# One weight load issued later, an addition moved from VectorE to GpSimd, four small transposes one block earlier, and one product of zeros fewer

## The chip, the cores and the metric

The kernel runs on one core of a Trainium2 chip. A core has five engines that run side by side, each with its own queue of instructions that it takes in order: TensorE (PE in the profile, with its weight loads shown apart as PEld), VectorE (DVE), ScalarE (ACT), GpSimd (POOL) and SyncE (SP). Transfers between the chip's main memory (HBM) and the on-chip memory are started by an instruction in one of these queues and then run on the core's 16 DMA engines. The metric is the time of one execution in microseconds (us) of the core.

## The reference

The inputs are x (8 batches of 1024 rows of 512), a condition row of 512 for each batch, and weights. Two layers are applied one after the other, each with a residual connection. Cut to what matters:

```python
ae = _layernorm(ada_emb, ln_g, ln_b)                  # 8 x 512
h = jax.nn.gelu(ae @ w1 + b1, approximate=False)      # 8 x 512
xw = h @ w2 + b2                                      # 8 x 8192
x_a, x_b = jnp.split(xw, 2, axis=-1)                  # each 8 x 512 x 8
layer = base_layer[None] + jnp.einsum('bdr,bkr->bdk', x_a, x_b)
x = x + (x + jnp.einsum('btc,bco->bto', x, layer))    # first layer
ys = y * scale                                        # y is the condition row
d = jax.lax.rsqrt(jnp.einsum('bi,io->bo', ys * ys, weight * weight) + EPS)
x = x + jnp.einsum('bsi,io->bso', x * ys[:, None, :], weight) * d[:, None, :]
```

The first layer is x(2I + base + a low-rank term), the second is x(I + diag(ys) W diag(d)), where I is the identity. So for each batch the kernel first makes one 512x512 matrix, P = (2I + base + low rank)(I + diag(ys) W diag(d)), and then multiplies the 1024 rows of x by it.

## The kernel before

**Tiling.** All 512-wide matrices are held as four chunks of 128 rows (one chunk for each set of 128 partitions). A product of two float32 matrices is made of three products in a shorter float format: each factor is split into a rounded part ("h", written by ScalarE as a copy or a scaled copy) and a rest ("l", written by VectorE as the difference), and h·h, h·l and l·h are summed in the accumulators.

**Stages.** A head of some 26 us loads the weights, makes the split of base (with 2I added) and of W, the layer norm of the condition, the gelu, and the first of the matrices. A middle part makes the other matrices while w2 streams in; then the main part multiplies x by them, 128 rows at a time, with the matrices for later batches made in between; the last batches use a seven-product scheme. TensorE works through all of these in one fixed order.

**What sets the order.** In the head nearly every instruction goes through a wrapper (`ve`, `se`, `sy` for VectorE, ScalarE, SyncE; `mm` and `turn` for TensorE; `pin` in general) that keeps each engine's instructions in the order in which they stand in the kernel. `nc.gpsimd` instructions are not wrapped unless `pin` is written around them. Waits between engines are put in by the framework from the data that the instructions read and write.

**The names that the change touches.**

- `w_sb` holds W. Its chunks 0 and 1 are loaded by two transfers from ScalarE's queue (lines 89 and 90), ahead of ScalarE's load of its function table and its first small activation (`root`, line 124). Chunks 2 and 3 come in one transfer from SyncE's queue.
- `b_raw` holds the transpose of base; chunks 0, 1 and then 2 with 3 are loaded from SyncE's queue. `sm` is a small block with the norm's gains, the transposed condition, and a 128x128 identity, `ident`.
- `twice_i(k)` (line 154) adds 2I to the diagonal 128x128 block of chunk k of `b_raw`. `round_b(k)` (line 158) is ScalarE's rounded copy `bh`, `rest_b(k)` VectorE's rest `bl`. `round_yw(k)` and `rest_yw(k)` do the same for diag(ys) W of batch 0 (tiles `nh` and `nl`, n0 in the kernel).
- For chunk 0 the rounding is done in three pieces: columns 128 to 255, 256 to 511, and last the diagonal block, columns 0 to 127 (lines 181 to 183). TensorE's first products take the four column blocks in the order 1, 2, 3, 0 (line 263), so that the fourth product is the first that needs the diagonal block.
- `keep_warm` (line 112) gives TensorE products of a tile of zeros, from about the start of the program until the first real operands are there; `WARM` says how many.
- `pg` are the four accumulators of the first product; `first_base(k, cs)` adds chunk k to the column blocks cs, three products for each. `RowsProduct(ysq, wsq, "v")` is a row product for d; it makes `pq_v`, ScalarE copies that to `q_v`, and `rv.turn()` transposes it (`pt_v`).
- `pa` receives the transposes of the normalised condition, `ae` (line 274; `ae` is a slice of the tile `drow`, and is called drow in the profile). VectorE makes `aeT` from it, and `aeT` feeds the next row product, `pq_z`.

Of the kernel before, what the change touches and what calls it, by code (L numbers as in the profile page):

```python
# [7 lines left out]
F32 = mybir.dt.float32  # L8
F32R = mybir.dt.float32r
AF = mybir.ActivationFunctionType  # L10
ALU = mybir.AluOpType
# [3 lines left out]
P = 128  # L15
# [8 lines left out]
D_EPS = 1e-8  # L24
SCALE = float(1.0 / D ** 0.5)
NFILL = 4
WARM = 12


@with_exitstack  # L30
def cond_resid_kernel(ctx: ExitStack, tc: tile.TileContext, small, cond, condrows, consts,
# [10 lines left out]
    nc = tc.nc  # L42
# [4 lines left out]
    def turn(*args):  # L47
        tc.keep_in_program_order(nc.tensor.transpose(*args))

    pin = tc.keep_in_program_order  # L50
# [13 lines left out]
    ve, se, sy = InOrder(nc.vector), InOrder(nc.scalar), InOrder(nc.sync)  # L64
# [12 lines left out]
    sp = setup.enter_context(tc.tile_pool(name="sp", bufs=1))  # L77
# [5 lines left out]
    w_sb = cp.tile([P, KC, D], F32, name="w_sb")  # L83
# [2 lines left out]
    xab = sp.tile([P, D], F32, name="xab")  # L86
    drow = sp.tile([P, D], F32, name="drow")
    cnd, ae = xab[:NB, :], drow[:NB, :]
    for k in range(2):
        se.dma_start(w_sb[:, k, :], weight[:, k, :])  # L90
    sy.dma_start(sm, small)
    for k in range(2):
        sy.dma_start(b_raw[:, k, :], baseT[:, k, :])
# [8 lines left out]
    ident = sm[:, 44:44 + P]  # L102
# [9 lines left out]
    def keep_warm(count):  # L112
        for _ in range(count):
            mm(warm.rearrange("p (a c) -> p a c", c=P), zero,
               zero.unsqueeze(1).to_broadcast([P, D // P, P]), start=True, stop=True)

    keep_warm(WARM)
    eps_d = cp.tile([P, 1], F32, name="eps_d")
# [3 lines left out]

    root = cp.tile([NB, 1], F32, name="root")
    se.activation(root, eps_l, AF.Sqrt)


    hT = sp.tile([P, KC, 2, 32], F32, name="hT")
    nc.gpsimd.memset(hT, 0.0)

    bh = cp.tile([P, KC, D], F32R, name="bh")  # L130
    bl = cp.tile([P, KC, D], F32R, name="bl")
# [13 lines left out]
    def round_yw(k):  # L145

        se.mul(n0[k][0], w_sb[:, k, :], ysT[:, k, 0:1])

    def rest_yw(k):
        h, l = n0[k]  # L150
        ve.scalar_tensor_tensor(l, w_sb[:, k, :], ysT[:, k, 0:1], h.bitcast(F32),
                                           ALU.mult, ALU.subtract)

    def twice_i(k):
        blk = b_raw[:, k, k * P:(k + 1) * P]
        ve.scalar_tensor_tensor(blk, ident, 2.0, blk, ALU.mult, ALU.add)

    def round_b(k, lo=0, hi=D, by=se.copy):
        (by(bh[:, k, lo:hi], b_raw[:, k, lo:hi]))
# [17 lines left out]

    ve.tensor_scalar_mul(ysT, condT, SCALE)
    twice_i(0)
    round_yw(0)  # L180
    round_b(0, P, 2 * P)
# [3 lines left out]
    rest_b(0)  # L185
    round_yw(1)
    twice_i(1)
    round_b(1)
    rest_yw(1)
# [11 lines left out]
    ve_l = sp.tile([NB, 1], F32, name="ve_l")  # L201
    ve.tensor_scalar(ve_l, mv[:, 1:2], 1.0, LN_EPS, ALU.mult, ALU.add)
    twice_i(2)
    twice_i(3)
    r, t = newton_rsqrt(ve_l, sd, [NB, 1], "l")
# [4 lines left out]
    def base_mms(ps, c, k, nhl, last):  # L210
        h, l = nhl
        for i, (s, m) in enumerate(((bh, h), (bh, l), (bl, h))):
            mm(ps, s[:, k, c * P:(c + 1) * P], m, start=(k == 0 and i == 0),
               stop=(last and k == KC - 1 and i == 2))
# [3 lines left out]
    def first_base(k, cs=range(KC)):  # L218
        for c in cs:
            base_mms(pg[c], c, k, n0[k], True)  # L220
# [43 lines left out]
            mm(pg[c], s[:, 0, c * P:(c + 1) * P], m, start=(i == 0), stop=False)  # L264
    first_base(1, (0, 1))
    round_yw(2)
    round_b(2)
    rest_yw(2)
    round_yw(3)
    rv = RowsProduct(ysq, wsq, "v")  # L270
    rv.keep()
    round_b(3)
    first_base(1, (2, 3))
    pa = misc.tile([P, KC, NB], F32, tag="misc", name="pa")
    for k in range(KC):
        turn(pa[:, k, :], ae[:, k * P:(k + 1) * P], ident[:NB, :NB])
    aeT = sp.tile([P, KC, 4, NB], F32, name="aeT")
    ve.tensor_mul(aeT, pa.unsqueeze(2).to_broadcast([P, KC, 4, NB]),
                  lng.unsqueeze(2).unsqueeze(3).to_broadcast([P, KC, 4, NB]))
# [915 lines left out]
```

## Time and profile before

| | |
|---|---|
| median of 3 runs | 294.32 us (294.32 to 295.01) |
| the profiled execution's own time | 294.56 us |
| its span in the profile | 292.8 us |
| TensorE busy | 287.9 us, 98% of the span |
| VectorE busy | 215.1 us, 73% |
| ScalarE busy | 175.0 us, 60% |
| GpSimd busy | 33.6 us, 11% |

The profile is of one execution. Its span runs from the first instruction to the last; the execution's own time is 1.76 us longer. "Busy" counts the time in which an engine works on an instruction, without the issue of transfers from SyncE and ScalarE. Ends of TensorE's products are modelled, so the distance between starts tells more than a duration.

### The profile page before, as it was taken

Reading aid. Unit: us, or ns where it says so; the run is one execution under the profiler, and the core shown is the slowest. Engines: PE = TensorE matmul, PEld = TensorE weight load, DVE = VectorE, ACT = ScalarE, POOL = GpSimd, SP = SyncE. Lnnn points to the kernel's source line nnn. Section 1 sums busy time; section 2 is a strip of 40 time slices with the busy share of each in tenths; the row PEclk is TensorE's granted clock in tenths of the full one; section 3 lists DMA queues with packets and bytes.
Section 4 is the critical chain, followed back from the end, with each engine's and each line's share of the span. In section 5 each row is a group of like instructions: output and inputs, shape, how many; then the busy total and the mean of one; then the engine's idle time right before and its main releaser. Section 6 shows DMA issues by size and latency. Waiting matters only on the chain.

```text
span 292.8 us, 4096 instructions
## 1 busy us (share of the span) xinstructions
PE 287.9 (98%) x1520; PEld 225.9 (77%) x1520; DVE 215.1 (73%) x299; ACT 175.0 (60%) x272; POOL 33.6 (11%) x72
## 2 busy tenths in 40 slices
PE   8999999999999999999999999999999999999995
PEld 3655566557877778888877888887888889999994
DVE  2789988989926999618799565325789976797912
ACT  4757254186858884748653575544658745846741
POOL 0011000202944551000023000000000000000000
PEclk9999999999999999999999999999999999999999
DMA  7999999993699784342428114252275870852334
GB/s 215 410 427 418 407 373 387 405 363 113 179 323 322 208 271 133 92 162 79 172 74 251 72 72 121 96 210 75 75 251 172 291 257 0 290 204 85 143 146 143
DMA packets 19924, 62.14 MB, mean 212 GB/s; under 512 B 2736, under 2 KB 4016, under 8 KB 15552
## 3 DMA queue, kind: packets, MB, share of 16 engines
q1 hardware_dynamic: 9504, 43.76, 40.2%
q10 hardware_dynamic: 6912, 12.32, 11.6%
q0 software_dynamic: 3488, 5.79, 7.5%
q8 instruction: 12, 0.20, 0.3%
q14 instruction: 8, 0.07, 0.1%
HBM read 44.02 MB, written 17.84 MB: 211 GB/s over the span
## 4 chain that ended last, share of the span: by engine, by line
PE 98%; DVE 0%; ACT 0%; issue 0%; ACTq 0%
PE po L45 42%; PE pp L45 20%; PE sw L45 9%; PE px L45 5%; PE sz L45 5%; PE pq L45 4%; PE pg L45 4%; PE sv L45 2%; PE warm L45 2%; PE pr L45 1%; PE pt_t L45 1%; PE ps_t L45 0%; PE pq_z L45 0%; PE pq_v L45 0%; ACT o L62 0%; DVE o L62 0%
## 5 line engine op out<-in xcount | busy, mean ns | idle before, releaser
L45 PE MATMUL po<-ph,xs 128*128 128x512 f32 x352 | 113.8, 393 | 0.0
L45 PEld LDWEIGHTS po<-ph,xs 128*128 128x128 f32 x352 | 66.1, 188 | 15.6 <-issue 1.7
L45 PE MATMUL po<-pl,xs 128*128 128x512 f32 x176 | 68.7, 390 | 0.0
L62 ACT COPY o<-po 128x512 f32<-128x512 f32 x44 | 25.9, 588 | 35.3 <-PE po L45 35.3
L45 PEld LDWEIGHTS po<-pl,xs 128*128 128x128 f32 x176 | 33.1, 188 | 6.7
L62 DVE TENSOR_TENSOR xs<-x,xs 128x1024 fp32r<-128x1024 f32 (+1 forms) x23 | 26.9, 1175 | 14.9 <-ACT xs L62 14.9
L62 DVE TENSOR_TENSOR nl_p<-n,nh_p 128x1024 fp32r<-128x1024 f32 x21 | 25.6, 1221 | 12.4 <-ACT nh_p L62 12.4
L62 ACT CAST nh_p<-n 128x1024 fp32r<-128x1024 f32 x21 | 22.1, 1053 | 13.0 <-DVE n L62 10.7
L62 ACT CAST xs<-x 128x1024 fp32r<-128x1024 f32 x22 | 23.0, 1056 | 3.4 <-DMA x<-in_x 3.4
L62 ACT COPY q<-pp 128x512 f32<-128x512 f32 x30 | 17.4, 586 | 8.8 <-PE pp L45 8.6
L539 POOL DMA_DIRECT2D fa<-kept_a x28 | 13.8, 512 | 58.4 <-PE pr L45 54.1
L45 PE MATMUL pp<-nh_p,sh 128*128 128x512 f32 x48 | 19.1, 397 | 0.0
L45 PE MATMUL pp<-nl_p,sh 128*128 128x512 f32 x48 | 18.8, 391 | 0.0
L45 PE MATMUL pp<-nh_p,sl 128*128 128x512 f32 x48 | 18.8, 391 | 0.0
L62 ACT CAST sh<-sraw 128x1024 fp32r<-128x1024 f32 (+1 forms) x14 | 12.9, 926 | 6.8 <-DVE sraw L62 6.8
L62 DVE SCALAR_TENSOR_TENSOR n<-w_sb,ysT,d 128x512 f32<-128x512 f32 x24 | 16.9, 746 | 0.0
L62 DVE TENSOR_TENSOR sl<-sraw,sh 128x1024 fp32r<-128x1024 f32 (+1 forms) x14 | 15.0, 1068 | 2.2 <-ACT sh L62 2.2
L62 DVE TENSOR_TENSOR pl<-q,ph 128x1024 fp32r<-128x1024 f32 (+1 forms) x10 | 11.1, 1116 | 7.0 <-ACT ph L62 6.9
L45 PE MATMUL px<-w,hT 128*32 128x512 f32 x128 | 15.6, 599 | 0.0
L62 ACT COPY o<-sw 128x512 f32<-128x512 f32 (+1 forms) x12 | 6.2, 518 | 15.4 <-PE sw L45 12.3
L62 DVE TENSOR_TENSOR q<-pr,q 128x512 f32<-128x512 f32 x14 | 8.8, 685 | 8.1 <-PE pr L45 8.0
L62 DVE TENSOR_TENSOR n<-n,n 128x1024 f32<-128x1024 f32 x12 | 14.5, 1222 | 0.1
(198 smaller groups left out, 576.9 us busy)
## 6 DMA issues: line engine op xcount, KB each, us to landing
w<-in_w SPq DMA_DIRECT2D x16, 1024.0 KB, 9.9
x<-in_x SPq DMA_DIRECT2D x16, 1024.0 KB, 5.5
out<-o ACTq DMA_DIRECT2D x44, 256.0 KB, 2.5
out<-o SPq DMA_DIRECT2D x8, 512.0 KB, 3.0
fa<-kept_a POOLq DMA_DIRECT2D x28, 64.0 KB, 2.8
ft<-kept_t POOLq DMA_DIRECT2D x28, 64.0 KB, 3.3
d<-d_out POOLq DMA_DIRECT2D x6, 256.0 KB, 7.7
w_sb<-in_w SPq DMA_DIRECT2D x1, 1024.0 KB, 8.4
```

The lines of the kernel that those rows point to most:

```text
L45: tc.keep_in_program_order(nc.tensor.matmul(*args, **kw))
L62: return lambda *a, **kw: pin(f(*a, **kw)) if InOrder.on else f(*a, **kw)
L539: nc.gpsimd.dma_start(fold[name, b][32 * c:32 * c + 32, :], kept[name, g][32 * i:32 * i + 32, :])
```

## The change

Four edits, all in the head:

- Of the two transfers of W on ScalarE's queue the second, chunk 1, is now issued behind the table load and the activation `root`.
- GpSimd makes a tile `two_i` = I + I once, and `twice_i` becomes an addition of that tile on GpSimd, for all four chunks. VectorE had done it with one multiply-and-add.
- The four transposes into `pa` are moved ahead of the last block (three products) of `first_base(1)`. In the text, `RowsProduct` and its copy `q_v` also move ahead of `round_b(2)` and `round_yw(3)`. On TensorE the row product stays where it was; on ScalarE the copy `q_v` now comes before the rounding of chunk 2.
- `WARM` goes from 12 to 11.

```diff
-WARM = 12
+WARM = 11
...
-    for k in range(2):
-        se.dma_start(w_sb[:, k, :], weight[:, k, :])
+    se.dma_start(w_sb[:, 0, :], weight[:, 0, :])
...
     se.activation(root, eps_l, AF.Sqrt)
+    se.dma_start(w_sb[:, 1, :], weight[:, 1, :])
...
     nc.gpsimd.memset(hT, 0.0)
+    two_i = sp.tile([P, P], F32, name="two_i")
+    pin(nc.gpsimd.tensor_tensor(two_i, ident, ident, ALU.add))
...
     def twice_i(k):
         blk = b_raw[:, k, k * P:(k + 1) * P]
-        ve.scalar_tensor_tensor(blk, ident, 2.0, blk, ALU.mult, ALU.add)
+        pin(nc.gpsimd.tensor_tensor(blk, blk, two_i, ALU.add))
...
     round_yw(2)
-    round_b(2)
     rest_yw(2)
-    round_yw(3)
     rv = RowsProduct(ysq, wsq, "v")
     rv.keep()
+    round_b(2)
+    round_yw(3)
     round_b(3)
-    first_base(1, (2, 3))
+    first_base(1, (2,))
     pa = misc.tile([P, KC, NB], F32, tag="misc", name="pa")
     for k in range(KC):
         turn(pa[:, k, :], ae[:, k * P:(k + 1) * P], ident[:NB, :NB])
+    first_base(1, (3,))
```

In the built program GpSimd's queue holds one instruction more than the text: between the clearing of `hT` and the making of `two_i` stands a reload of GpSimd's library of code (library number 0). It waits for nothing. The program before has no such instruction: there GpSimd only clears, copies and issues transfers.

## The prediction

> **What bounds the kernel now.** I read the page first, then the chain that ended last, then the first 15 us in order of time, engine by engine, because the diff touches nothing later. The page:
>
> ```profile
> span 292.8 us, 4096 instructions
> PE 287.9 (98%) x1520; PEld 225.9 (77%) x1520; DVE 215.1 (73%) x299; ACT 175.0 (60%) x272; POOL 33.6 (11%) x72
> PE 98%; DVE 0%; ACT 0%; issue 0%; ACTq 0%
> ```
>
> TensorE carries 98% of the span and 98% of the chain. So nothing done on another engine shortens the kernel unless TensorE starts earlier or loses an idle moment, and whatever lets TensorE idle in the head is added to the end almost whole: the 265 us behind the head have no slack to give it back. The chain in order of time, for the head:
>
> ```profile
> 0.99 5.30 PE warm L45 x12
> 6.29 4.50 PE pg L45 x18
> 10.79 0.99 PE pq_v L45 x8
> ...
> 13.38 0.34 PE pa L48 x4
> 13.72 0.60 PE pt_v L48 x4
> 14.32 0.15 issue
> 14.47 1.07 PE pq_z L45 x8
> ```
>
> TensorE runs without a break from 0.99, and the only idle moment here that the diff can reach is the 0.15 ahead of pq_z, where the transposes feed aeT. The other engines in that stretch, in order of time:
>
> ```profile
> 0.73 0.31 POOL L128 MEMSET hT<- 128x256 f32 x1 [0.29 <-POOLq L1187]
> 1.66 1.28 ACT L62 ACT_TABLE_LOAD   x1 [1.66 <-PEq L1187]
> 3.86 0.18 DVE L62 TENSOR_SCALAR ysT<-sm 128x32 f32<-128x32 f32 x1 [2.92 <-DMA sm<-in_small]
> 5.69 0.81 ACT L62 CAST bh<-b_raw 128x128 fp32r<-128x128 f32 x3 [0.59 <-DMA b_raw<-in_baseT]
> 6.40 0.72 ACT L62 ACTIVATE nh<-w_sb,ysT 128x512 fp32r<-128x512 f32 x1
> 7.48 0.62 ACT L62 CAST bh<-b_raw 128x512 fp32r<-128x512 f32 x1 [0.36 <-DVE b_raw L62]
> 10.21 0.49 DVE L62 SCALAR_TENSOR_TENSOR b_raw<-sm,b_raw 128x128 f32<-128x128 f32 x2 [0.21 <-DMA b_raw<-in_baseT]
> 15.60 0.40 POOL L745 CAST onesb<-cst 128x256 fp32r<-128x256 f32 x1 [14.55 <-DMA cst<-in_consts]
> ```
>
> and the weight loads of TensorE between 5.5 and 7.4:
>
> ```profile
> 6.04 1.05 PEld L45 LDWEIGHTS pg<-nh,bh 128*128 128x128 f32 x4 [0.66 <-ACT bh L62]
> 7.13 0.42 PEld L45 LDWEIGHTS pg<-nl,bh 128*128 128x128 f32 x2
> ```
>
> Base chunk 0 lands at about 5.65. ScalarE then rounds its three pieces; looked at one by one they start at 5.69, 5.90 and 6.20 (0.29 us for the last, the diagonal block). The first four real weight loads start at 6.04, 6.35, 6.63 and 6.90. The first two follow the first two pieces within 0.06; the fourth, which needs the diagonal block, comes 0.41 after that piece is done. From there TensorE goes at 0.23 a product.
>
> **Fewer zeros.** The twelve zero products start 0.43 apart, the last at 5.65, so TensorE is free at 6.08, just when the first rounded piece is there. Without one it is free at 5.65. What that is worth hangs on base chunk 0 landing earlier: nothing if it does not, 0.43 at most.
>
> **W chunk 1 later.** ScalarE's two issues took 0.89, the table load 1.28, root 0.20. The second issue moves from 1.2 to about 0.73 + 0.45 + 1.28 + 0.20 = 2.66, 1.5 later; its own 0.43 on ScalarE falls into that engine's 1.23 wait for W chunk 0. The pair landed 4.1 after issue in the mean, the first 3.6, so the second 4.6, at 5.8. It would now land between 5.8 (if the queue had held it back anyway) and 7.3. Its reader is the scaled copy nh at 6.40, behind which bh, four squares, sd and the norm stand on ScalarE. At 7.3 the copy of base chunk 1 would start at 8.0 instead of 7.48, and VectorE's two rests would end at about 9.45, where TensorE wants the second one at 9.46. So the delay costs nothing to 0.1, and covers itself with the two rests; with TensorE 0.4 ahead it would eat that gain. In return chunk 0 and 1 of base, on SyncE's queue, share the DMA engines with 256 KB less for 1.5 us: base chunk 0 lands up to half a microsecond earlier, or not at all.
>
> **Transposes sooner.** pa moves up by three products, 3 x 0.23 = 0.7. Its input, drow, ended at 12.05; the transposes would be wanted at 13.30 - 0.7 = 12.6, so it is there. aeT (0.61 for both steps) then runs under the three products, and the 0.15 ahead of pq_z goes: -0.15. Next late would be q_v, but the copy moves up on ScalarE. The four additions that VectorE loses (0.29, 0.28 and 0.49 for two) free 1.06 us on an engine that is not on the chain; they bring drow forward by up to 0.2, worth nothing more.
>
> **2I by GpSimd.** This is the part that decides. GpSimd's queue in the built program is: clear hT, reload of the code library, two_i, the four additions. ScalarE's third piece waits for the first addition, and in ScalarE's queue stand behind it nh(1), bh(1), the four squares, sd and all that follows; on TensorE the fourth product waits, and the whole kernel behind it; VectorE's bl(0) needs all three pieces. The reload begins when hT is cleared, at 0.73 + 0.31 = 1.04. Call its length L. An addition on GpSimd is not in the trace: the bounds are VectorE's 128x128 addition (0.29) and twice GpSimd's 256-element cast (0.80); I take the cast itself, 0.40, as two inputs of 128 are the same number of elements read. Then two_i is made at 1.04 + L + 0.40, the first block at 1.04 + L + 0.80, the third piece takes 0.05 + 0.29, and the fourth weight load follows 0.05 later: 2.23 + L. It stood at 6.90. So the reload is hidden up to L = 4.7, and above that every microsecond of it is a microsecond of TensorE. ScalarE's later work does not add to this: its 0.36 wait for VectorE's addition (at 7.48) disappears, since GpSimd's second addition is done 0.4 after the first.
>
> L itself no row of before shows. The lower bound is the only reload of an engine's tables, ScalarE's 1.28. The upper is the longest fetch in the head: cst, 136.5 KB, 9.9 from issue to landing. Between them lie the loads of this stretch, which take longer the more traffic there is: sm 3.1, W chunk 0 3.6, base chunk 0 4.5, W chunks 2 and 3 6.4, base chunks 2 and 3 7.3, w1 8.4. The DMA engines are busy at a share of 0.85 in the fourth microsecond and about 1.0 from the fifth on, so a reload that starts at 1.04 runs through the filling queues. [...] L = 8.4 puts the fourth weight load at 10.63, a stall of 3.73.
>
> [...]
>
> **Sum**, against the profiled execution: 294.56 + 3.73 (stall) - 0.15 (idle ahead of pq_z) - 0 (the zero product, since TensorE waits anyway) = 298.14. The median of the runs is 0.24 below the profiled execution, so I predict 297.9.
>
> **Rivals.**
>
> (1) *The reload is hidden or does next to nothing* (L under 4.7, for instance because library 0 is there already). For it: ScalarE's table load is only 1.28 and sm lands at 3.8, so up to L = 2.8 GpSimd waits for data anyway. Against it: the full DMA queues. Then TensorE gains 0 to 0.43 at the start and 0.15 at pq_z: 294.56 - 0.24 - 0.15 to 0.58, that is 293.7 to 294.2; if W chunk 1 is late at the same time, 294.3. This is not slower, and decides at L = 4.7.
>
> (2) *A short stall*, L from 4.7 to 6.4 (W chunks 2 and 3): a stall of 0 to 1.73, 294.2 to 295.9. [...]
>
> (3) *The stall, and a slow TensorE behind it.* At the start the zero products are 0.43 apart, and 0.23 is reached only at the fourth real product, some 5.5 us after the first; the PEclk row shows 1.00 all the while, so the slowness is seen in the spacing alone. If an idle TensorE of about 4 us falls back to that state, the next 12 to 13 products go at 0.43 until 5.5 us have passed: 12.5 x 0.20 = 2.5 more, 300.4. Against it: nowhere behind the start does TensorE idle long enough for the trace to show such a fall. [...]
>
> (4) *GpSimd and VectorE hinder each other* while both read two operands; bounded by one addition each, 0.4 to 0.8 together, inside the range below.
>
> **Chances.** The long stall at full speed 0.46 (296 to 299.4, L = 6.5 to 9.9), the long stall with a slow TensorE 0.18 (298 to 302), the short stall 0.12, hidden 0.24. The likeliest is the first, 297.9, with 296.0 to 299.4 as its own range. The range over the cases: from 293.8, which leaves out only the last 0.1 of the hidden case, to 301.0, which leaves out the slow TensorE with the longest reload. A difference of 0.3%, 0.88 us, is about what a measurement of this kernel can tell from none. Faster by that much needs more than the 0.58 that all gains add up to: 0.03. Within it: the hidden case and the part of the short one with L below 5.7: 0.26. Slower: 0.71.
>
> **What the profile after would show.** If right: two_i starts at about 9.4 although sm landed at 3.8; the third bh piece waits for POOL's b_raw until 10.2; PEld pg shows an idle of 3 to 4 us ended by ACT bh, at the fourth pg product; nh(1), bh(1) and the squares follow without a wait; no idle ahead of pq_z; the span behind pq_z as before. Products 0.43 apart after the stall would be rival 3. If two_i starts before 5.7, rival 1 or 2 holds and only the start (6.04 or 5.65 for the first pg weight load) and the place of nh(1) remain to be read. The prediction is wrong if GpSimd's reload is cheap, which no row of before excludes.

## The result, and the profile after

The changed kernel takes 294.0 us in the median of 20 runs (293.67 to 294.64), the kernel before 294.44 us in the median of 20 runs beside them (294.11 to 295.52). The ratio is 0.9984, with a 95% interval of 0.9977 to 0.9991: 0.47 us faster, between 0.26 and 0.68. The prediction was 297.9 us, slower by more than 1%. What happened is its rival 1, for which it gave 293.7 to 294.2 us and a chance of 0.24: GpSimd's reload held nothing up.

The page of the kernel after begins:

```profile
span 291.9 us, 4100 instructions
PE 286.3 (98%) x1519; PEld 225.2 (77%) x1519; DVE 214.8 (74%) x295; ACT 175.0 (60%) x272; POOL 35.9 (12%) x77
PE 96%; DMA 2%; ACT 0%; DVE 0%; SPq 0%; ACTq 0%; issue 0%
```

TensorE does one product less, VectorE four instructions less and GpSimd five more. The span is 0.9 shorter than in the profile before; the profiled execution itself took 293.74 us, against 294.56. TensorE is still the bound, but the chain now begins with a transfer, 2% of the span: with eleven zeros TensorE is done before base chunk 0 is there.

GpSimd's part, and what was to wait for it, in order of time from the kernel after (start, duration, engine, line, operation, and in brackets the idle time ahead and what ended it):

```profile
1.18 1.28 ACT L62 ACT_TABLE_LOAD   x1 [1.18 <-PEq L1190]
1.24 0.39 ACTq L62 DMA_DIRECT2D w_sb<-in_weight  x1
2.48 0.20 ACT L62 ACTIVATE root<-eps_l 8x1 f32<-8x1 f32 x1
4.09 0.39 POOL L130 TENSOR_TENSOR two_i<-sm 128x128 f32<-128x128 f32 x1 [3.04 <-DMA sm<-in_small]
5.75 0.90 ACT L62 CAST bh<-b_raw 128x128 fp32r<-128x128 f32 x3 [0.54 <-DMA b_raw<-in_baseT]
5.87 0.46 POOL L158 TENSOR_TENSOR b_raw<-b_raw,two_i 128x128 f32<-128x128 f32 x1 [1.38 <-DMA b_raw<-in_baseT]
6.10 0.83 PEld L45 LDWEIGHTS pg<-nh,bh 128*128 128x128 f32 x4 [1.56 <-ACT bh L62]
```

`two_i` starts at 4.09, and what it waited for is the transfer of `sm`, not a reload. The first addition of 2I waits for base chunk 0 and is done at 6.33, while ScalarE is still at the second piece; the three pieces go without a break (0.90 for three) and so do TensorE's first four weight loads (0.83 for four, the fourth at about 6.74). The idle of 3 to 4 us ahead of the fourth is not there. The second thing to see is the second line: W chunk 1 was issued at 1.24, while the table load ran, and ahead of `root`, though it stands behind both in ScalarE's queue. In the kernel before it went out at about 1.2 too.

So where does the gain come from? The chain of the kernel after in order of time (start, duration, what):

```profile
1.16 4.56 DMA b_raw<-in_baseT
...
10.64 1.00 PE pq_v L45 x8
...
14.21 0.99 PE pq_z L45 x8
15.21 1.59 PE pg L45 x6
...
17.23 0.69 PE pg L45 x3
17.93 0.44 PE pdr L48 x4
18.37 1.40 PE pg L45 x6
...
25.36 2.99 PE pq L45 x12
```

and the same stretch of the kernel before, from where the prediction's lines of it end:

```profile
15.54 1.59 PE pg L45 x6
...
17.57 0.70 PE pg L45 x3
18.27 0.13 issue
18.40 0.63 PE pdr L48 x4
19.03 1.39 PE pg L45 x6
...
26.02 2.98 PE pq L45 x12
```

`pdr` is a set of four transposes that follows the last line the prediction showed. Starts against starts: at `pq_v` after is 0.15 ahead (10.64 against 10.79); from there to the `pg` behind `pq_z` it takes 4.57 instead of 4.75, another 0.18; from the three `pg` ahead of `pdr` to the six behind it, 1.14 instead of 1.46, another 0.32; 0.01 is rounding. All of it is 0.66 at `pq`. The other 0.24 of the difference in the spans lies behind the head, where the diff touches nothing, and is not traced to anything.

The 0.32 at `pdr` was in no step of the prediction. `pdr` transposes `dT`, and `dT` is the end of a row of VectorE instructions that begins with `aeT`. VectorE before:

```profile
13.76 0.29 DVE L62 TENSOR_TENSOR aeT<-pa,sm 128x128 f32<-128x128 f32 x1 [1.04 <-PE pa L48]
...
17.56 0.69 DVE L62 TENSOR_TENSOR dT<-r_d,t_d 128x512 f32<-128x512 f32 x1
```

and after:

```profile
12.95 0.27 DVE L62 TENSOR_TENSOR aeT<-pa,sm 128x128 f32<-128x128 f32 x1
...
16.90 0.69 DVE L62 TENSOR_TENSOR dT<-r_d,t_d 128x512 f32<-128x512 f32 x1
```

In both profiles VectorE's row from `aeT` to `dT` runs in the order of the kernel, 3.80 us from start to start before and 3.95 after. Before, it stood idle for 1.04 until `pa` was there, and everything behind `aeT`, down to `dT`, was that much later. Now `aeT` is 0.81 earlier and `dT` 0.66, and `pdr` finds its input.

### The profile page after: what moved, and what is told of

Read it like the earlier page. It is cut to its first block, busy times and chain, and to the rows that moved or that the text cites. A ratio compares the mean times of both kernels' runs of the same rounds, so it can differ in the third digit from the quotient of the medians.

```text
span 291.9 us, 4100 instructions
## 1 busy us (share of the span) xinstructions
PE 286.3 (98%) x1519; PEld 225.2 (77%) x1519; DVE 214.8 (74%) x295; ACT 175.0 (60%) x272; POOL 35.9 (12%) x77
## 2 busy tenths in 40 slices
DMA packets 19924, 62.14 MB, mean 213 GB/s; under 512 B 2736, under 2 KB 4016, under 8 KB 15552
## 4 chain that ended last, share of the span: by engine, by line
PE 96%; DMA 2%; ACT 0%; DVE 0%; SPq 0%; ACTq 0%; issue 0%
PE po L45 42%; PE pp L45 20%; PE sw L45 9%; PE px L45 5%; PE sz L45 5%; PE pg L45 4%; PE pq L45 4%; PE sv L45 2%; DMA b_raw<-in_baseT 2%; PE pr L45 1%; PE pt_t L45 1%; PE ps_t L45 0%; PE pq_v L45 0%; PE pq_z L45 0%; ACT o L62 0%; DVE o L62 0%
## 5 line engine op out<-in xcount | busy, mean ns | idle before, releaser
L62 DVE TENSOR_TENSOR sl<-sraw,sh 128x1024 fp32r<-128x1024 f32 (+1 forms) x14 | 14.9, 1067 | 2.2 <-ACT sh L62 2.2
```

The lines of the kernel that those rows point to most:

```text
L62: return lambda *a, **kw: pin(f(*a, **kw)) if InOrder.on else f(*a, **kw)
```

## The experiments

Two theories stood at the start. The first: the gain is the earlier transposes alone; the reload costs nothing because library 0, the one it asks for, is there already. The rival: the reload does take some microseconds and hides in the 3 us in which GpSimd waits for `sm` anyway (it would be hidden up to L = 4.7), or the other edits share in the gain. All ratios are against runs of the kernel before on the same chip. They are worked out from all the runs of both kernels, so they can differ a little from the quotient of the two medians.

### One edit alone, three times, and one undone

The third edit alone, in the kernel before (run a1):

```diff
     round_yw(2)
-    round_b(2)
     rest_yw(2)
-    round_yw(3)
     rv = RowsProduct(ysq, wsq, "v")
     rv.keep()
+    round_b(2)
+    round_yw(3)
     round_b(3)
-    first_base(1, (2, 3))
+    first_base(1, (2,))
     pa = misc.tile([P, KC, NB], F32, tag="misc", name="pa")
...
+    first_base(1, (3,))
```

> Only the third edit: the transposes into pa one block sooner, and with them q_v's copy ahead of the rounding of chunk 2. Theory 1 (the transposes carry the gain): the norm's tile reaches VectorE 0.8 us sooner, so the d chain ends sooner; no idle ahead of pq_z (0.15 before), no wait of pdr for dT, pdr about 0.44 from start to the next pg instead of 0.76; in all 0.45 to 0.55 us off, a ratio of 0.998. Theory 2 (the gain is VectorE's 1.06 us freed by GpSimd): little here, at most the 0.15 ahead of pq_z, ratio 0.9995.

293.94 us against 294.4, ratio 0.9986 (0.9975 to 0.9998). The whole gain is there without the other three edits. Its chain, at the two places that moved:

```profile
14.33 0.99 PE pq_z L45 x8
...
18.05 0.44 PE pdr L48 x4
```

No idle ahead of `pq_z`, and `pdr` takes 0.44 with none ahead, as in the kernel after.

The addition on GpSimd alone (run a2):

```diff
     nc.gpsimd.memset(hT, 0.0)
+    two_i = sp.tile([P, P], F32, name="two_i")
+    pin(nc.gpsimd.tensor_tensor(two_i, ident, ident, ALU.add))
...
-        ve.scalar_tensor_tensor(blk, ident, 2.0, blk, ALU.mult, ALU.add)
+        pin(nc.gpsimd.tensor_tensor(blk, blk, two_i, ALU.add))
```

> Only the second edit: 2I added by GpSimd. Theory 1: no change beyond 0.1 us either way; aeT still waits for pa as before, so VectorE's freed time is worth nothing; two_i starts when sm is there, at 3.9 to 4.1. Theory 2: 0.3 to 0.5 us off. If the reload of GpSimd's code costs time only in some executions, the runs spread to 297 or more here.

294.45 us, ratio 1.0003 (0.9991 to 1.0014). `two_i` starts at 4.17, and the chain keeps both of the idle moments of the kernel before, ahead of `pq_z` and of `pdr`:

```profile
14.75 0.15 issue
...
18.70 0.13 issue
```

So freeing VectorE of four additions (1.06 us) moves nothing: its row begins when `pa` is there, whatever VectorE did before. That step of the prediction holds.

The first and fourth edits alone (run a3), that is the W chunk and the zeros:

```diff
-WARM = 12
+WARM = 11
...
-    for k in range(2):
-        se.dma_start(w_sb[:, k, :], weight[:, k, :])
+    se.dma_start(w_sb[:, 0, :], weight[:, 0, :])
...
     se.activation(root, eps_l, AF.Sqrt)
+    se.dma_start(w_sb[:, 1, :], weight[:, 1, :])
```

> Only the first and fourth edits: chunk 1 of W behind the table load, eleven zero products. Theory 1: nothing within 0.1 us; the first real weight load at 6.0 to 6.1 as in both profiles, since base chunk 0 lands at 5.65 to 5.73, and the issue of chunk 1 at 1.2 all the same, while the table load runs. Theory 3 (the earlier start carries the gain): 0.2 to 0.4 us off.

294.41 us, ratio 0.9996 (0.9987 to 1.0005). W chunk 1 goes out at 1.24 here too. In its profiled execution base chunk 0 landed at 6.32 and TensorE's first real product was at 6.69. Between profiled executions of kernels that issue their loads in this order that landing lies anywhere from 5.58 to 6.32, so single profiles are compared from a fixed point inside the head, as above, and the runs decide. (The profiled executions of a2 and a3 were the slowest of their twelve, 295.77 and 294.99 us.)

The third edit undone, the other three kept (run a4):

```diff
     round_yw(2)
+    round_b(2)
     rest_yw(2)
+    round_yw(3)
     rv = RowsProduct(ysq, wsq, "v")
     rv.keep()
-    round_b(2)
-    round_yw(3)
     round_b(3)
-    first_base(1, (2,))
+    first_base(1, (2, 3))
...
-    first_base(1, (3,))
```

> The changed kernel without its third edit. Theory 1: the gain is gone, ratio 0.9995 to 1.0005 against the kernel before, with pdr waiting for dT again. Theories 2 and 3: the gain stays, ratio 0.998 to 0.999.

294.61 us, ratio 1.0004 (0.9993 to 1.0014): the gain is gone. This run also names the chain that the prediction had missed, since it goes through VectorE in it:

```profile
13.29 0.35 PE pa L48 x4
...
13.67 0.30 DVE aeT L62
...
15.55 0.41 DVE s_v L62 x4
...
17.48 0.70 DVE dT L62
...
18.32 0.63 PE pdr L48 x4
```

From `pa` the work goes to `aeT`, over two instructions that only stand in between in VectorE's queue (`bl` at 14.21 and `nl` at 14.89), to `s_v`, `dT` and `pdr`. Here GpSimd's first addition, beside VectorE, took 0.66 instead of 0.46, and TensorE's fourth weight load waited 0.20 for the piece behind it.

### Where the copy q_v stands

The prediction held that `q_v` would be the next late thing if its copy did not move up. The transposes moved, the copy left where it was (run b3):

```diff
     round_b(3)
-    first_base(1, (2, 3))
+    first_base(1, (2,))
     pa = misc.tile([P, KC, NB], F32, tag="misc", name="pa")
...
+    first_base(1, (3,))
```

> Only the transposes into pa moved, q_v's copy left where it was on ScalarE. Theory 1 in its narrow form (the norm's tile being sooner is all): the same gain as with the copy moved, ratio 0.9985, since q_v ended at 12.6 before and is wanted at about 13.4. If the copy's place matters: pt_v waits for it, and the gain is 0.1 to 0.4 us smaller.

293.91 us against 294.43, ratio 0.9983 (0.9972 to 0.9993). The same gain; `pt_v` starts at 13.71 and the copy, at 12.05 for 0.56, is done 1.1 ahead of it. Its place is worth nothing. The whole of the kernel's gain is two lines: `first_base(1, (2, 3))` split, with the four transposes between its halves.

### What a reload costs

To see the reload without GpSimd's wait for `sm`, the kernel after was given a clear and an addition of two spare tiles ahead of `two_i`, which wait for nothing (run b1); the sum is not used. In the built program the reload of library 0 then stands between the two.

```diff
     nc.gpsimd.memset(hT, 0.0)
+    probe = [sp.tile([P, P], F32, name=f"probe_{i}") for i in range(2)]
+    pin(nc.gpsimd.memset(probe[0], 0.0))
+    pin(nc.gpsimd.tensor_tensor(probe[1], probe[0], probe[0], ALU.add))
     two_i = sp.tile([P, P], F32, name="two_i")
```

> The changed kernel with a GpSimd addition of a cleared tile to itself ahead of two_i; it waits for no transfer, so it starts when the reload of library 0 is done. If the reload is skipped because that library is there: it starts within 0.2 us of the second clearing, at about 1.3 to 1.5. If the reload is real but was hidden under two_i's wait for sm: somewhere from 1.6 to 4. The probe's output is used by nothing.

One run: 293.86 us, against 294.43. GpSimd, in order of time:

```profile
0.98 0.20 POOL L130 MEMSET probe<- 128x128 f32 x1
1.27 0.39 POOL L131 TENSOR_TENSOR probe<-probe 128x128 f32<-128x128 f32 x1
```

The clear ends at 1.18 and the addition starts at 1.27: the reload costs at most 0.1 us. It was not hidden behind the transfer of `sm` (`two_i` starts at 4.45); it does next to nothing. To see whether that is because the library is there already, another one was put between (run b2): the spare addition became a broadcast across partitions, which needs library 1, so that the built program loads library 1 ahead of it and library 0 behind it. Its output is not used either.

```diff
-    pin(nc.gpsimd.tensor_tensor(probe[1], probe[0], probe[0], ALU.add))
+    pin(nc.gpsimd.partition_broadcast(probe[1], probe[0]))
```

> As the probe before, but the probe is a broadcast over partitions, which needs library 1, so that two_i needs a real reload of library 0. [...] If changing libraries is cheap always: two_i at 4.1 as before, no change of time.

One run: 309.35 us, 14.9 above the kernel before. GpSimd:

```profile
0.97 0.21 POOL L130 MEMSET probe<- 128x128 f32 x1
10.73 0.43 POOL L131 PARTITION_BROADCAST probe<-probe  x1 [9.55 <-issue]
18.95 0.39 POOL L133 TENSOR_TENSOR two_i<-sm 128x128 f32<-128x128 f32 x1 [7.79 <-issue]
```

and TensorE's weight loads:

```profile
20.25 0.29 PEld L45 LDWEIGHTS pg<-nh,bh 128*128 128x128 f32 x1 [13.48 <-ACT bh L62]
20.42 1.62 PEld L45 LDWEIGHTS pg<-nl,bh 128*128 128x128 f32 x4
...
23.68 0.19 PEld L45 LDWEIGHTS pg<-nh,bh 128*128 128x128 f32 x1
```

The two exchanges that really took place cost 9.55 and 7.79 us in this stretch. The record of the broadcast between the two, 0.43, is rough, as the profile's spans on GpSimd are; so how the 17.8 us from the end of the clear (1.18) to `two_i` (18.95) are split between the two exchanges and the broadcast is not shown. No instruction shows the exchange, only an idle that nothing ends ("issue"), and the rows of the DMA queues hold the same packets and bytes as in the kernel after (19924 and 62.14 MB in all). The stall has the place that the prediction gave it: two pieces are rounded and three products made, and the fourth weight load waits 13.48 for the third piece. Behind the stall the products are about 0.4 apart for some 3.3 us (eight weight loads from 20.42 to 23.68) before they reach 0.23: rival 3's slow TensorE. Here the granted clock shows it too. It is this row of the page, one digit for each 7.7 us of the span:

```profile
PEclk9659999999999999999999999999999999999999
```

In finer steps the granted clock reads 1.00 until about 9.8, 2.6 us after TensorE fell idle, then 0.50 until about 23.4, and 1.00 from there. Against the kernel after, the first `px` comes at 34.59 instead of 19.77, 14.8 later: 13.5 for the fourth weight load (20.25 against 6.74) and 1.3 for the fifteen products from there to `pq_v` (5.21 against 3.90). For code that is there already the cost was at most 0.1 (b1).

### Zeros

The prediction put the zero product at nothing, as TensorE waits for base chunk 0 anyway. If zeros only fill a wait, six would do (run d3, the kernel after with six):

```diff
-WARM = 11
+WARM = 6
```

> The changed kernel with six zero products in place of eleven. If the zeros only fill time until base chunk 0 is there: no change, ratio 0.9984, first real weight load at 6.0 and real products 0.23 apart soon after. If they bring TensorE to full speed: the zeros end at 3.6, TensorE idles 2.4 us, and the real products start 0.43 apart for 2 to 5 us, that is 1 to 2.5 us on the time, ratio 1.002 to 1.007.

296.05 us against 294.53, ratio 1.0054 (1.0038 to 1.0069), some 2 us above the kernel after. Weight loads of TensorE:

```profile
6.06 1.36 PEld L45 LDWEIGHTS pg<-nh,bh 128*128 128x128 f32 x4 [3.24 <-ACT bh L62]
7.51 1.61 PEld L45 LDWEIGHTS pg<-nl,bh 128*128 128x128 f32 x4
...
10.62 0.19 PEld L45 LDWEIGHTS pg<-nh,bh 128*128 128x128 f32 x1
```

The first real product is where it was (6.06, against 6.10), but the products are 0.4 apart until 10.62, and the eighteen take 6.34 us instead of 4.54. So the zeros are not there to fill a wait: they bring TensorE to its narrow spacing of 0.23, and fewer of them cost nothing only while enough are left (eleven in a3, but not six here). In this run the granted clock reads 1.00 all the while, so that the slow start is seen in the spacing alone, unlike the slow stretch behind the stall of b2. How much work brings the narrow spacing is not shown as one figure. Behind the six zeros, 2.6 us of work at 0.43 each, the wide spacing lasts 4.6 us (6.06 to 10.62), and behind the stall of b2 3.3 us; the narrow spacing is there 2.9 us after the first zero product in the profiles of b1 and e1 (at 3.9) and only 5.9 us after it in that of the kernel before (at 6.9). How long an idle time brings the wide one back is shown once: in b2 the granted clock fell 2.6 us after the last product.

### What the first edit may have been meant to do

The second W load did not move in the change. If it is put where it does move, behind base chunk 0 on SyncE's queue, does TensorE start earlier, and is that kept? First in the kernel with the third edit alone (twelve zeros, run c1):

```diff
-    for k in range(2):
-        se.dma_start(w_sb[:, k, :], weight[:, k, :])
+    se.dma_start(w_sb[:, 0, :], weight[:, 0, :])
     sy.dma_start(sm, small)
     for k in range(2):
         sy.dma_start(b_raw[:, k, :], baseT[:, k, :])
+        if k == 0:
+            sy.dma_start(w_sb[:, 1, :], weight[:, 1, :])
```

> The transposes' edit on the kernel before, and chunk 1 of W issued on SyncE's queue behind chunk 0 of base, so that it really comes later. If the start is bound by base chunk 0 and this shares the DMA engines with W chunk 1: base chunk 0 lands 0.3 to 1.0 us sooner (5.6 before), the first real weight load is at 5.0 to 5.7, and the time falls by 0.2 to 0.5 us more than by the transposes alone, ratio 0.997. If base chunk 0 is not held up by W chunk 1: the first weight load stays at 6.0 and the ratio at 0.9985.

294.18 us against 294.43, ratio 0.9991 (0.998 to 1.0003). One of its twelve runs took 473.91 us, at a granted clock of 0.56 where the others had 1.00, and is left out of the ratio. Base chunk 0 landed at about 5.26, 0.3 or more ahead of any profile with the old order and inside the half microsecond that the prediction gave as the most, but the twelve zeros held TensorE until 6.29. Then with ten zeros (run d1):

```diff
-WARM = 12
+WARM = 10
```

> The transposes' edit, chunk 1 of W on SyncE's queue behind base chunk 0, and ten zero products in place of twelve, so that TensorE is free at about 5.2 at the latest. If the start is bound by base chunk 0 once the zeros are out of the way: first real weight load at 5.6 (chunk 0 landed at 5.26 with this order), the norm's chain without a wait, 0.3 to 0.45 us below the transposes alone, ratio 0.997. If the norm's tile or the squares now bind the row product and the transposes: the gain is eaten there, ratio 0.9985 again, with an idle ahead of pq_v or pa.

294.05 us against 294.53, ratio 0.999 (0.9971 to 1.0009): not better than the third edit alone. TensorE starts at 5.44, 0.66 ahead of the kernel after, and has lost that lead by `pa` (12.67, against 12.53):

```profile
5.44 4.79 PE pg L45 x18
10.23 1.46 PE pq_v L45 x8
```

Of the 0.66, 0.25 is gone by `pq_v` (10.23 against 10.64): with ten zeros the first four real weight loads take 1.19 instead of 0.83, TensorE's slow spacing. Then `pq_v` takes 1.46 instead of 1.00: its last inputs are the squares of W chunks 2 and 3, and ScalarE waits 0.32 for their transfer. The next was to issue base chunk 0 ahead of `sm` as well (run d2):

```diff
-    sy.dma_start(sm, small)
     for k in range(2):
         sy.dma_start(b_raw[:, k, :], baseT[:, k, :])
         if k == 0:
+            sy.dma_start(sm, small)
             sy.dma_start(w_sb[:, 1, :], weight[:, 1, :])
```

> As the run with ten zero products, and base chunk 0 also issued ahead of the small block sm. Base chunk 0 lands at 4.7 to 5.0, sm 0.3 to 0.6 later than 3.9; the scaled copy of W chunk 0 then starts at 4.4 to 4.7 and ends at 5.1 to 5.4, and the first real weight load is at 5.5: level with the other order or 0.1 better. If sm is late by a microsecond, the scaled copy is, and it is slower than the other order.

294.0 us, ratio 0.9992 (0.9979 to 1.0005). Now `sm` lands at 5.10, 3.9 after its issue, the scaled copy that needs it ends at 6.06, and TensorE starts at 6.30. Then the start of d1 was kept and the row product moved one block of three products later, behind its squares, with `sd` ahead of the fourth square (run e1):

```diff
-    for k in range(KC):
+    for k in range(3):
         square_w(k)
...
+    square_w(3)
...
-    first_base(1, (0, 1))
+    first_base(1, (0, 1, 2))
...
-    first_base(1, (2,))
     pa = misc.tile([P, KC, NB], F32, tag="misc", name="pa")
```

> As the run with ten zero products and chunk 1 of W behind base chunk 0, and the two waits that ate its gain taken away: the row product pq_v stands behind one more block of the first product (0.7 us later on TensorE), and ScalarE makes the norm's deviation ahead of the fourth square (0.4 us sooner). If those waits were the only cover: first real weight load at 5.3 to 5.6, no idle ahead of pq_v and pa, pdr without a wait, 0.3 to 0.5 us below the transposes alone, ratio 0.997. If q_v, now 0.7 us later, is late for pt_v, or dT for pdr: an idle there of 0.1 to 0.5 us, and the ratio stays at 0.9985.

294.18 us against 294.57, ratio 0.9991 (0.9982 to 1.0). The squares are no longer late, but there is now an idle of 0.77 ahead of `pa`. The addition on VectorE, in order of time:

```profile
10.79 0.50 DVE L62 SCALAR_TENSOR_TENSOR b_raw<-sm,b_raw 128x128 f32<-128x128 f32 x2 [1.27 <-DMA b_raw<-in_baseT]
```

and the chain of the same run:

```profile
11.97 0.77 issue
12.74 0.38 PE pa L48 x4
```

VectorE waits 1.27 for base chunks 2 and 3 in order to add 2I, and behind that addition stands the rest of the norm, whose result `pa` transposes. That is a place at which GpSimd's additions could be worth something, so they were put in, once into e1 (run f1) and once into d1 (run f2):

```diff
+    two_i = sp.tile([P, P], F32, name="two_i")
+    pin(nc.gpsimd.tensor_tensor(two_i, ident, ident, ALU.add))
...
-        ve.scalar_tensor_tensor(blk, ident, 2.0, blk, ALU.mult, ALU.add)
+        pin(nc.gpsimd.tensor_tensor(blk, blk, two_i, ALU.add))
```

> The earlier start with ten zero products, chunk 1 of W behind base chunk 0, pq_v one block later and the norm's deviation ahead of the fourth square, and now 2I added by GpSimd. If it was the addition to base chunk 2 in VectorE's queue (1.27 us of waiting for its transfer) that held the norm: the reciprocal follows sd at about 10.4, drow ends at 11.8, pa has no idle ahead of it, the time falls to 293.5 to 293.8, ratio 0.997 to 0.998. If GpSimd's additions are worth nothing: 0.77 us of idle ahead of pa as without, ratio 0.999.

> The same without the two moves of pq_v and of the deviation: start at 5.3 to 5.6, 2I by GpSimd. The squares wait for W chunks 2 and 3, so pq_v idles 0.3 to 0.5 us; pa no longer does. Ratio 0.998 to 0.999 if GpSimd's additions free the norm; 0.999 to 1.000 if the first of them (0.4 to 0.7 us where VectorE's was 0.29) delays the start as much.

294.04 us against 294.41, ratio 0.9992 (0.9979 to 1.0006), and 294.37, ratio 1.0 (0.9992 to 1.0009). In the first the idle ahead of `pa` falls from 0.77 to 0.15, but 0.38 of that is only `pq_v` ending later; `pa` itself starts 0.24 sooner (12.50 against 12.74). VectorE no longer waits for base chunk 2: its reciprocal follows ScalarE's `sd` and starts at 10.64 instead of 11.20, so the wait in VectorE's queue did hold it. Of these 0.56, 0.31 are lost again in the small operations behind it, one of which takes 0.40 beside GpSimd's additions instead of 0.15. And base chunk 1 landed at 7.38 in this run, ScalarE waited 1.41 for GpSimd's addition to it, and TensorE for ScalarE; in the second ScalarE's wait was 1.21. Two lines of the first:

```profile
7.94 0.62 ACT L62 CAST bh<-b_raw 128x512 fp32r<-128x512 f32 x1 [1.41 <-POOL b_raw L159]
...
10.64 0.15 DVE L62 RECIPROCAL r_l<-sd 8x1 f32<-8x1 f32 x1 [0.18 <-ACT sd L62]
```

So an earlier start of 0.5 to 0.7 us was had four times (d1, e1, f1, f2) and kept in none of them. In d1 a part of it went into slow first products. For the rest, and in the other three, the next transfer in the row was what came late: W chunks 2 and 3, base chunks 2 and 3, base chunk 1. What order of the loads would keep the lead, if any does, stays open. None of the versions beats the kernel after or the third edit alone beyond what the intervals tell.

## Why the prediction was wrong, point by point

**The reload (L = 8.4, a stall of 3.73).** This is the step that failed, and nearly the whole of the miss of 3.9 us. Its sum took for granted that the reload fetches code, and chose its length between bounds from rows of transfers. No run shows the 8.4 for this reload: in its place b1 showed at most 0.1, as it asks for the library that is there already (with another one put between, in b2, 7.79). For a reload that does exchange the code the place of the stall was right (the fourth weight load), and the size was near: 8.4 against 9.55 and 7.79 measured. The size is luck in part: 8.4 was the time of w1's transfer, and the DMA queues show no transfer for an exchange. The condition was named, in rival 1, but judged by its length alone. Nothing else in the program asks for another library, so there was nothing to exchange; the prediction named that and gave it too little weight. That the time lies in the range of rival 1 (293.7 to 294.2) is luck in part too: its range counts up to 0.43 for an earlier start, of which a3 shows nothing, and leaves out the 0.32 at `pdr`.

**W chunk 1.** The step "the second issue moves from 1.2 to 2.66" failed. The issue went out at 1.24, beside the table load; what moved is the table load, from 1.66 to 1.18. Its cost of nothing was right for another reason than the one given.

**Transposes sooner, -0.15.** The gain at `pq_z` is 0.18, so the size was right. The step "next late would be q_v" failed: next late was `dT`, and it was late in the kernel before already, by an idle of 0.13 and a slower `pdr`, one line below the last line of the chain that was shown. That it would come forward with `aeT` is another 0.32. The gain tied to the edit is then 0.50, against 0.47 measured. The remaining 0.15 at the start of `pq_v` is taken as chance. It comes from the first four real weight loads, which take 1.05 in the profile of the kernel before, where TensorE reaches the spacing of 0.23 only behind them, and 0.83 in that of the kernel after, where it has it from the first. They are fast (0.83 to 0.84) in a1, b3 and a3 too, and slow (1.22 and 1.19) in c1 and d1; so the third edit stands in both groups, and the other three edits show no gain in their runs (a2, a3, a4). That reading is argued from the profiles, not tested.

**Fewer zeros, 0.** Right in size: a3 shows no difference. The argument covered only the wait; what the zeros are for was shown by the run with six of them.

**GpSimd's additions.** Taken at 0.40. `two_i` took 0.39 with nothing beside it, and an addition into `b_raw` 0.46 with VectorE idle (the second of f1); beside two-operand work of VectorE they took up to 0.77 (the second of a4). The other way round, VectorE's `nl` took 0.93 to 0.97 beside an addition (after, f1, f2) and 0.73 to 0.75 elsewhere. That is rival 4, at the size it was given (0.4 to 0.8 together at most), and a2 shows no cost to the kernel (0.9991 to 1.0014).

**A slow TensorE behind the stall (rival 3).** It came in b2, at half the size: 1.3 for the fifteen products instead of 2.5. The 2.5 rested on slow products until 5.5 us after the first (in the trace before, 5.9: 6.90 less 0.99); behind the stall they lasted 3.3.

**Freed VectorE time worth nothing.** Right (a2).

## What to carry to other kernels

An instruction that an operation brings along, such as a reload, is priced in two questions, whether it has anything to do and how long it takes: here the answers were 0.1 us and 8 to 10 us, and a probe that waits for nothing tells them apart in one run each. When one input is made to come sooner, follow its engine's queue on to everything behind it, for all the places at which it was late, and not only the first idle moment. And before an earlier start is paid for, look which transfer is read next: in this head, in which the DMA engines are busy at a share of about 1.0 (1.03 from 4 to 5 us, 1.02 from 6 to 11 and 1.01 from 11 to 20 in the kernel after), the lead gained on one load was given back to a following one each time.

## What the runs showed of the hardware that was not expected

- A transfer issued by ScalarE went out at 1.24, although a table load (1.18 to 2.46) and an activation (2.48) stood ahead of it in the same queue.
- The exchange of GpSimd's code took 9.55 and 7.79 us under the traffic of the head (one run, with the broadcast's record between them), is shown by no instruction and by no more packets in the DMA queues (19924, as in the kernel after); asking for code that is there took at most 0.1.
- GpSimd and VectorE slowed each other where both read two operands: 0.46 became 0.52 to 0.77 on GpSimd, 0.73 to 0.75 became 0.93 to 0.97 on VectorE. A small step of the norm with one operand took 0.14 beside GpSimd's additions (f1) and without them (e1), the one ahead of it, with two, 0.40 and 0.15.
- TensorE at its slow spacing (0.4 instead of 0.23 a product) is seen in the granted clock behind the stall of b2, where it reads 0.50, and not at the start of the program, where it reads 1.00 with the zeros 0.43 apart.
